# Regrouping one search's VectorE work into fewer slots in step 1 of an adjacency-attention kernel

## Chip, core and metric

The kernel runs on one core of a Trainium2 chip. The metric is the time of one execution on the device in microseconds (us); the time of a kernel is the median of its runs. Work is issued to five engines, each with its own queue taken in order: TensorE (PE, with its weight loads shown apart as PEld), VectorE (DVE), ScalarE (ACT), GpSimd (POOL) and SyncE (SP, which here only starts DMAs).

## What is computed

Two layers over 2708 nodes with 256 features. The part that the change touches is in layer 0, which does this twice (step 0, step 1), with `Xf = Xa = X` at first:

```python
R = S + eye;  R = R / R.sum(-1, keepdims=True)      # S: the 2708 x 2708 adjacency
for n in range(2):
    A  = top_p_attention(Xa, W1, W2, W3)            # softmax rows, kept to 90% of their mass
    Xf = R @ Xf
    Xa = A @ Xa
    Z  = Z + Xf @ U1[n].T + Xa @ U2[n].T
# then a layernorm; layer 1 is a 4-head masked attention over the same graph, and a layernorm
```

`top_p_attention` sorts each row of probabilities in descending order, keeps entries until the sum before an entry reaches 0.9, sets the others to zero and divides by the sum that is left. So every row needs its own threshold.

## The kernel before

**Tiles and loops.** The 2708 rows are cut into 22 tiles, 16 of 128 rows and 6 of 110. In each of the two steps a loop over the 22 tiles (`step`) does the product `A @ Xa` of one tile: in six groups of up to four column blocks, PE transposes the block of the tile's probabilities `e` (L269), ACT copies the result out of PSUM as `eT` (L274), and PE multiplies it with the values into the bank `att` (L287). After each group `between` calls `slot` once. So there are six slots to a tile, and a slot is the unit of the hand-written order.

**What a slot issues** (`slot`, in this order): one more part of each search that is under way, the oldest search first; one part of each row-wise job that is under way (`doing`: layernorms and sums of finished rows; a layernorm here is L136, L138, L140 and L144 on DVE and L142 on POOL); the start of a new search, where one is due; and 11 or 12 matmuls of the *walk*. PE, ACT, DVE and POOL are in manual order (`engines`, in `tc.manual_schedule`): each does its instructions in the order in which the generators issued them. SP is not in that set: a planner of the language puts its DMAs in order, by when it expects each to be ready.

**The walk** (`walks`) is `R @ Xf` for both steps. It is one long stream that starts at the end of step 0's attention and ends at the end of step 1's. For each of 11 pairs of tiles it makes seven products of 11 matmuls each (L1136), which are combined later. The products share two PSUM banks in most of the stream. Each product must be read out before the next but one can use its bank: products 1, 2 and 5 by ACT (L1144, L1150, L1152), products 6, 7, 4 and 3 by DVE (L1146, L1148, L1154, L1156). A readout is issued with the last matmul of its product, so on DVE it stands behind the search work of its slot. L1158 and L1160 are two short reciprocals of the walk.

**A search** (`search`) finds the threshold of one tile. Each `yield` in it ends its part for the present slot. In step 1 its parts are, with the slots counted from the search's start:

- slots 0 and 1, `scores`: logits on PE (L798), exponentials on ACT (L817); a few sums on POOL
- slots 1 to 5, `survey`: four passes over `e` on ACT (L840, 2.64 us each) and short POOL instructions between them (L849 to L872)
- slot 6, `bound`: ten short DVE instructions, then one pass over 2708 columns (L905) that writes `scr`
- slots 7 and 8, `candidates`: 28 MAX8 instructions on DVE (L920), 14 in each slot, which take the eight largest of each of 28 pieces
- slot 9, first part of `settle`: the sort (L933 to L940: six MAX8 and five MATCH_REPLACE8 over 224 candidates) and the sums (L942 to L949)
- slot 10: counts of ties (L958 to L979)
- slot 11: seven MATCH_REPLACE8 over `e` (L986), which write `key`
- slot 12: the last masking of `e` (L989) and a reciprocal (L992); then the tile is ready

A new search starts every tile, in the slot after group 4 (the fifth of the tile), for the tile three ahead. So three searches overlap, one of them at slot k + 6 when another is at slot k. The last masking of a tile is issued in the fifth slot of the tile before it, and the first transposes of the masked tile come in the PE queue right behind that slot's walk matmuls. Before the loop of step 1 starts, a stretch without attention issues 15 slots with 14 walk matmuls each, in which the first three searches of step 1 start.

In step 0 the same functions run with `s == 0`: no `survey`, no `bound`, no ties.

Of the kernel before, what the change touches and what calls it, by code (L numbers as in the profile page):

```python
# [47 lines left out]
def kernel(  # L48
# [506 lines left out]
    def fast_layer0(ep, adjp):  # L555
# [17 lines left out]
        parts = (CHUNKS_0, CHUNKS_1)  # L573
# [258 lines left out]
        def new(name, m):  # L832
            return small.tile([P, 1], F32, name=name)[:m]
# [78 lines left out]
        def candidates(s, t, src):  # L912

            m = rows[t]
            size = -(-N // parts[s])
            cand = sortp.tile([P, CHUNKS_1, 8], F32, name="cand")[:m, : parts[s]]
            for n in range(parts[s]):
                if n == parts[s] // 2:
                    yield
                nc.vector.max(cand[:, n, :], src[:m, n * size : min(N, (n + 1) * size)])  # L920
            return cand

        def settle(s, t, e, cand, tau):

            m = rows[t]  # L930
            want = sorted_[s]
            _, nxt, most, above, left = (f[:m, t : t + 1] for f in facts[s])
            nc.vector.tensor_reduce(most, cand[:, :, 7], axis=AX.X, op=ALU.max)  # L933
            flat = cand.rearrange("p n k -> p (n k)")
            work = sortp.tile([P, CHUNKS_1 * 8], F32, name="work")[:m, : parts[s] * 8]
            top = sortp.tile([P, SORTED_0], F32, name="top")[:m, :want]
            for k in range(0, want, 8):
                nc.vector.max(top[:, k : k + 8], work if k else flat)
                if k + 8 < want:
                    nc.vector.match_replace(work, top[:, k : k + 8], work if k else flat, 0.0)  # L940
            sums = sortp.tile([P, SORTED_0], F32, name="sums")[:m, :want]
            nc.vector.tensor_tensor_scan(sums, top, top, 0.0, op0=ALU.add, op1=ALU.max)  # L942
            nc.vector.scalar_tensor_tensor(
                sums, sums, tau, top, op0=ALU.subtract, op1=ALU.is_ge, accum_out=left
            )
            nc.vector.tensor_tensor_reduce(
                sums, sums, top, 1.0, 0.0, op0=ALU.mult, op1=ALU.max, accum_out=nxt
            )
            nc.vector.tensor_scalar(  # L949
                sums, top, nxt, None, op0=ALU.is_gt, op1=ALU.add, accum_out=above  # L950
            )
            key = e
            if s:
                yield

                need = new("need", m)
                upto = small.tile([P, SEGS], F32, name="upto")[:m]
                nc.vector.tensor_add(need, above, left)  # L958
                nc.vector.tensor_scalar(
                    need, need, -1.0, float(want), op0=ALU.mult, op1=ALU.add  # L960
                )
                nc.vector.tensor_scalar(work, flat, nxt, None, op0=ALU.is_equal)
                nc.vector.tensor_reduce(
                    haves[:m, t], work.rearrange("p (s k) -> p s k", s=SEGS),
                    axis=AX.X, op=ALU.add,
                )
                nc.vector.tensor_tensor_scan(
                    upto, haves[:m, t], haves[:m, t], 0.0, op0=ALU.add, op1=ALU.max
                )
                nc.vector.tensor_sub(upto, haves[:m, t], upto)  # L970
                nc.vector.tensor_scalar(wants[:m, t], upto, need, None, op0=ALU.add)
                few = sortp.tile([P, SEGS, 8], F32, name="few")[:m]
                none = sortp.tile([P, SEGS, 8], F32, name="none")[:m]
                nc.vector.tensor_tensor(
                    few, place[:m].unsqueeze(1).to_broadcast([m, SEGS, 8]),
                    wants[:m, t].unsqueeze(2).to_broadcast([m, SEGS, 8]), op=ALU.is_lt,
                )
                nc.vector.tensor_scalar(none, few, -1.0, None, op0=ALU.add)
                nc.vector.scalar_tensor_tensor(  # L979
                    few, few, nxt, none, op0=ALU.mult, op1=ALU.add  # L980
                )
                yield
                key = wk.tile([P, N], F32, name="scr")
                for k in range(SEGS):
                    cut = slice(k * seg, min(N, (k + 1) * seg))
                    nc.vector.match_replace(key[:m, cut], few[:, k, :], e[:m, cut], 3e38)  # L986
            yield
            den, rden = new("den", m), new("rden", m)
            nc.vector.scalar_tensor_tensor(  # L989
                e[:m], key[:m], nxt, e[:m], op0=ALU.is_gt, op1=ALU.mult, accum_out=den  # L990
            )
            nc.vector.reciprocal(rden, den)  # L992
            return rden

        def search(s, t):

            e, z, tau = yield from scores(s, t)
            if s:
                seen = yield from survey(t, e, z, tau)
                src, rest = bound(t, e, z, tau, *seen)  # L1000
            else:
                src, rest = e, tau
            yield
            cand = yield from candidates(s, t, src)
            yield
            ready[t] = e, (yield from settle(s, t, e, cand, rest))
# [897 lines left out]
```

## Time and profile before

| | |
|---|---|
| median of 3 runs | 1517.05 us (1516.17 to 1520.15) |
| the profiled execution | 1516.33 us, of which the span is 1514.5 us |
| mean granted TensorE clock | 0.994 |
| PE busy over the span | 1485.1 us (98%) |
| DVE busy | 1282.9 us (85%) |
| ACT busy | 808.8 us (53%) |
| POOL busy | 596.7 us (39%) |

By stretch, from the span's start: step 0's attention runs from about 66 us to 430 us; the stretch between the steps to about 500 us; step 1's attention to 1178 us; layer 1 to the end. Busy time of 100 us in three stretches of step 1:

| stretch | PE | DVE | ACT | POOL |
|---|---|---|---|---|
| 500 to 600 us | 99.97 | 82.11 | 58.24 | 24.93 |
| 800 to 900 us | 99.41 | 91.32 | 63.29 | 51.93 |
| 1000 to 1100 us | 98.65 | 91.92 | 63.38 | 48.64 |

An engine's share of the whole span says little about one stage; the table by stretch and the list of who waits for whom say more. The layernorms of finished rows run on DVE and POOL only from about 800 us on, since they need the second walk.

### The profile page before, as it was taken

The numbers are of one execution on the slowest core, as the hardware profiler recorded it, in microseconds if no ns is written. First come the engines' busy times: TensorE is split into PE (matmuls) and PEld (weight loads), VectorE is DVE, ScalarE is ACT, GpSimd is POOL, SyncE is SP. The second block draws the span as 40 slices with busy tenths as digits, with TensorE's granted clock in tenths as the row PEclk, the third lists the DMA queues.
The fourth block names the chain that finished last, engine by engine and source line by source line (L and its number), as shares of the span: only waits on it lengthen the run. The fifth ranks groups of instructions, "written<-read, shape, count | busy, mean of one in ns | idle before, by whom it ended". The sixth has DMA issues, their size and how long they took to land. (4 is left out here: it accounts for less than half of the span.)

```text
span 1514.5 us, 30074 instructions
## 1 busy us (share of the span) xinstructions
PE 1485.1 (98%) x10547; PEld 1068.2 (71%) x10547; DVE 1282.9 (85%) x3750; ACT 808.8 (53%) x1535; POOL 596.7 (39%) x978
## 2 busy tenths in 40 slices
PE   9999999999999999999999999999989999999996
PEld 5477777777788889888888888888879333333343
DVE  4589999999516978888899988999986998999996
ACT  3444544454336456655665666665643444456474
POOL 0066775765023322222355544544552210045133
PEclk9999999999999999999999999999999999999998
DMA  6478988885048555545665555655455555334331
GB/s 182 142 251 271 292 260 256 257 234 177 12 136 264 165 173 180 165 131 146 183 192 157 172 170 173 181 168 161 149 167 142 153 143 164 101 106 133 89 106 53
DMA packets 214265, 255.92 MB, mean 169 GB/s; under 512 B 41921, under 2 KB 180317, under 8 KB 214105
## 3 DMA queue, kind: packets, MB, share of 16 engines
q1 hardware_dynamic: 203638, 245.31, 54.4%
q10 hardware_dynamic: 10467, 8.60, 1.8%
q8 instruction: 85, 1.39, 0.4%
q14 instruction: 75, 0.61, 0.1%
HBM read 190.03 MB, written 62.44 MB: 167 GB/s over the span
## 5 line engine op out<-in xcount | busy, mean ns | idle before, releaser
L274 ACT COPY eT<-tr 128x512 f32<-128x512 f32 (+5 forms) x264 | 141.7, 537 | 229.4 <-PE tr L269 226.6
L840 ACT ACTIVATE junk<-e,minus,rth 128x2708 bf16<-128x2708 f32 (+1 forms) x88 | 232.9, 2646 | 48.3 <-POOL rth L872 47.5
L287 PE MATMUL att<-ba,eT 128*128 128x256 f32 (+3 forms) x968 | 231.5, 380 | 0.0
L287 PE MATMUL att<-xm,eT 128*128 128x256 f32 (+3 forms) x968 | 230.8, 379 | 0.3 <-ACT xa L1374 0.3
L1691 PE MATMUL acc<-pt,v 128*32 128x512 f32 (+3 forms) x2112 | 217.0, 543 | 0.4
L1679 DVE SCALAR_TENSOR_TENSOR pt<-e,tj,blk 128x1024 f32<-128x1024 f32 (+3 forms) x176 | 184.1, 1110 | 6.0 <-ACT blk L251 2.7
L287 PEld LDWEIGHTS att<-ba,eT 128*128 128x128 f32 (+3 forms) x968 | 170.2, 187 | 21.6
L287 PEld LDWEIGHTS att<-xm,eT 128*128 128x128 f32 (+3 forms) x968 | 169.5, 186 | 22.0 <-ACT xa L1374 0.7
L1136 PEld LDWEIGHTS walk<-xe,blk 128*128 128x128 f32 (+1 forms) x1386 | 164.3, 187 | 13.7 <-issue 10.7
L1136 PE MATMUL walk<-xe,blk 128*128 128x128 f32 (+3 forms) x1386 | 173.3, 275 | 0.5 <-ACT u_sb L1144 0.4
L1691 PEld LDWEIGHTS acc<-pt,v 128*32 128x32 f32 (+1 forms) x2112 | 71.4, 110 | 126.6 <-issue 91.5
L269 PE MATMUL tr<-ident,e 128*128 128x128 f32 (+3 forms) x968 | 147.1, 271 | 2.0 <-ACT eT L274 1.4
L817 ACT ACTIVATE e<-lg 128x1024 f32<-128x1024 f32 (+3 forms) x112 | 106.6, 957 | 67.3 <-PE lg L798 64.7
L269 PEld LDWEIGHTS tr<-ident,e 128*128 128x128 f32 (+3 forms) x968 | 113.4, 139 | 32.8 <-issue 14.0
L1136 PE MATMUL walk<-xm,blk 128*128 128x128 f32 (+3 forms) x1034 | 131.6, 277 | 3.0 <-DVE xw L1156 1.7
L1136 PEld LDWEIGHTS walk<-xm,blk 128*128 128x128 f32 (+3 forms) x1034 | 124.8, 188 | 13.2 <-issue 6.5
L1701 PE MATMUL acc<-pt,sb 128*32 128x512 f32 (+3 forms) x1056 | 113.8, 542 | 0.0
L1679 DVE SCALAR_TENSOR_TENSOR pt<-r,tj,blk 128x1024 f32<-128x1024 f32 (+1 forms) x88 | 109.9, 1312 | 1.3 <-PE acc L1701 0.5
L920 DVE MAX8 cand<-e 128x8 f32<-128x170 f32 (+1 forms) x352 | 86.0, 320 | 24.5 <-ACT e L817 16.2
L250 ACT ACTIVATE blk<-blk 128x1024 f32<-128x1024 f32 (+3 forms) x66 | 63.3, 960 | 77.8 <-DMA blk<-in_adjT_dram 71.7
L920 DVE MAX8 cand<-scr 128x8 f32<-128x97 f32 (+1 forms) x616 | 102.8, 244 | 0.0
L824 POOL TENSOR_TENSOR fact<-zp 128x1 f32<-128x1 f32 (+1 forms) x44 | 40.0, 909 | 136.0 <-ACT e L817 135.9
(298 smaller groups left out, 2488.4 us busy)
## 6 DMA issues: line engine op xcount, KB each, us to landing
blk<-in_adjT_dram SPq DMA_DIRECT2D x68, 512.0 KB
blk<-S SPq DMA_DIRECT2D x48, 512.0 KB
blk<-D SPq DMA_DIRECT2D x24, 512.0 KB
blk<-in_adjT_dram SPq DMA_DIRECT2D x26, 440.0 KB
D<-blk SPq DMA_DIRECT2D x16, 512.0 KB
S<-scr SPq DMA_DIRECT2D x16, 512.0 KB
S<-blk SPq DMA_DIRECT2D x16, 512.0 KB
xm<-S SPq DMA_DIRECT2D x16, 512.0 KB
```

Source lines behind the costliest of these rows:

```text
L250: nc.scalar.activation(bar, bar, AF.Sign)
L269: nc.tensor.transpose(tr[: rows[t], q, :m], e[:m, off[t] : off[t + 1]], ident[:m, :m])
L274: copy(eT[:k, : len(grp), :m], tr[:k, : len(grp), :m])
L287: nc.tensor.matmul(acc, eT[: rows[t], q, :m], value(t), start=(t == 0), stop=(t == NT - 1),)
L817: nc.scalar.activation(halves[:m, :, c0 : c0 + w], lg[:m, :, :w], AF.Exp, accum_out=zp[:m, n : n + 1],)
L824: nc.gpsimd.tensor_add(z, zp[:m, 0:1], zp[:m, 1:2])
L840: nc.scalar.activation(junk[:m], e[:m], func, scale=rth, bias=minus1[:m], accum_out=acc)
L920: nc.vector.max(cand[:, n, :], src[:m, n * size : min(N, (n + 1) * size)])
L1136: nc.tensor.matmul(ac, blk[:k, j, :], MOVING[name](j, k, w), start=start and j == 0, stop=j == PAIRS - 1, skip_group_check=True,)
L1679: nc.vector.scalar_tensor_tensor(pt[:k, :gw], targets[g][h // 2][:k, h % 2, :gw], tj[:k, j, h : h + 1], bar, op0=ALU.max, op1=ALU.mult,)
L1691: nc.tensor.matmul(acc[h // 2][c][to : to + SIDE, :w], v[j][:k, h, o : o + SIDE], probs[n][h][:k, c0 : c0 + w], **at,)
L1701: nc.tensor.matmul(acc[2][c][h * SIDE : (h + 1) * SIDE, :w], sb[:k, j, h : h + 1].to_broadcast([k, SIDE]), probs[n][h][:k, c0 : c0 + w], **at,
```

## The change

```diff
@@ candidates
             for n in range(parts[s]):
-                if n == parts[s] // 2:
+                if n == parts[s] // 2 and not s:
                     yield
                 nc.vector.max(cand[:, n, :], src[:m, n * size : min(N, (n + 1) * size)])
@@ settle
                 if k + 8 < want:
                     nc.vector.match_replace(work, top[:, k : k + 8], work if k else flat, 0.0)
+            if s:
+                yield
             sums = sortp.tile([P, SORTED_0], F32, name="sums")[:m, :want]
             nc.vector.tensor_tensor_scan(sums, top, top, 0.0, op0=ALU.add, op1=ALU.max)
@@ settle
             key = e
             if s:
-                yield
-
                 need = new("need", m)
```

In step 1 the 28 MAX8 of a search are issued in one slot instead of two; a slot ends between the sort and the sums; and no slot ends between the sums and the counts of ties. The parts from slot 6 on become:

| slot of the search | before | after |
|---|---|---|
| 6 | bound | bound |
| 7 | 14 MAX8 | 28 MAX8 |
| 8 | 14 MAX8 | sort |
| 9 | sort, sums | sums, ties |
| 10 | ties | MATCH_REPLACE8 over `e` |
| 11 | MATCH_REPLACE8 over `e` | last masking |
| 12 | last masking | (ready) |

No instruction is added or removed on any engine. The order on PE, ACT and POOL stays as it was, and so does that of the DMAs that ACT starts. The order on DVE changes as in the table. The planner of SP's queue also moves some DMAs past each other, all from step 1's attention on, but for one pair before it: stores of finished rows (L1322) and loads of row tiles (L1089, L1090, L1094) change places with loads of walk blocks (L693, L681); and at the end of step 1 the first three loads of layer 1's values (L1667, tiles 8, 9 and 10) come ahead of its first mask load (L248) and of two loads of `e` (L228), and wait for DVE there. Step 0 keeps its slots. Lines are numbered as in the kernel before.

## The prediction

> **What bounds the kernel.** I read the page first: busy time, then the slices.
>
> ```profile
> PE 1485.1 (98%) x10547; PEld 1068.2 (71%) x10547; DVE 1282.9 (85%) x3750; ACT 808.8 (53%) x1535; POOL 596.7 (39%) x978
> ...
> PE   9999999999999999999999999999989999999996
> ...
> DVE  4589999999516978888899988999986998999996
> ```
>
> PE has no room nearly everywhere, and DVE is second, with the least room in the second half of step 1 (slices of 37.9 us; 20 to 30 are 757 to 1174 us). The change leaves PE's instructions and their order alone. So it can only gain what PE waits now, and what follows from such waits. The list of PE's waits from 500 to 1180 us has it whole (columns: engine and line, what it waited for, us in total, times, longest):
>
> ```profile
> PE walk L1136 <- DVE xw L1154: 3.5, 1, 3.5
> PE walk L1136 <- DVE xw L1156: 1.7, 1, 1.7
> PE tr L269 <- ACT eT L274: 1.4, 2, 0.8
> PE lg L798 <- ACT cs L184: 1.2, 2, 1.0
> PE walk L1136 <- ACT u_sb L1144: 1.1, 2, 0.7
> PE tr L269 <- DVE e L989: 0.6, 1, 0.6
> PE walk L1136 <- DVE u_sb L1148: 0.6, 1, 0.6
> PE lg L174 <- ACT xT L170: 0.6, 1, 0.6
> ```
>
> With 0.2 left out these are 10.7 us. DVE has a part of 6.4 us: one wait for the masking, and three for a bank of the walk that DVE had not read out. The same list before 500 us has one more, 1.3 us for L1146 at 485 us. The largest comes at the end, in the timeline from 1112 to 1136 us (start, us, engine):
>
> ```profile
> 1122.02 3.03 DVE L989 SCALAR_TENSOR_TENSOR e<-scr,fact,e 110x2708 f32<-110x2708 f32 x1
> ...
> 1128.10 3.47 DVE L905 SCALAR_TENSOR_TENSOR scr<-e,hi 110x2708 f32<-110x2708 f32 x1
> ...
> 1132.21 0.28 DVE L1154 TENSOR_TENSOR xw<-walk,u_sb 110x128 f32<-110x128 f32 x1
> ```
>
> The last masking of one search and the pass of the next one's bound stand in the same slot; the readout L1154, whose product had ended at 1124.36, stands behind both. PE sat from 1129.02 to 1132.54. Last, the granted clock by stretch (stretch, its length, PE busy, clock, DMA):
>
> ```profile
> 1128.00:1132.00 4.00, 1.02 (x10) 1.00 0.86 228
> 1132.00:1134.00 2.00, 1.46 (x7) 0.55 1.09 300
> 1134.00:1136.00 2.00, 2.00 (x7) 0.59 0.69 221
> 1136.00:1138.00 2.00, 2.00 (x14) 1.00 0.05 15
> ```
>
> After that wait PE got half its clock: (0.45 + 0.41) x 2 us / 0.5 = 3.4 us of it, which is 1.7 us lost. The 1.74 us wait that ended at 500.03 has the same behind it (0.69, 0.50 and 0.96 in the 2 us stretches from 500 us: 3.4 us). The 1.27 us wait at 485 us has not.
>
> [...]
>
> **The change, part by part.** Nothing is added, so the account is one of places in DVE's queue. Lengths of the parts, from DVE's timeline around 500 us, where no layernorms lie between: masking 3.24 us, bound 5.13, 14 MAX8 2.34, sort 5.08, sums 1.13, ties 2.47, MATCH_REPLACE8 over e 3.80. Together 25.5. Taking slots modulo six, since a search at slot 12 meets the next at slot 6, DVE got per slot 8.4, 2.3, 2.3, 6.2, 2.5, 3.8 and will get 5.1, 4.7, 5.1, 3.6, 3.8, 3.2. A tile takes PE about 30 us (equal logits follow at 30.2 us at 557 and 587), so a slot is some 5 us: the heap of 8.4 goes. Seen from the start of the bound's slot, DVE's work up to the end of each slot changes by -3.3, -0.9, +1.9, -0.7, +0.6, 0. Readouts behind the bound come earlier; those behind the sort come later.
>
> I laid DVE's rows out in the new order with these lengths, each readout no earlier than its product's end, each layernorm no earlier than POOL's part had been, and the bound no earlier than its last ACT pass had been, and compared each end with the time at which PE starts the next product in that bank.
>
> *Between the steps* (468 to 511 us DVE never idles). After the bound's readout at 473.8, 28 MAX8 end at 478.4; L1154, which was at 476.06, comes then and PE, which wants the bank at 478.05, waits 0.7. Sort, sums and ties follow before L1146: 478.44 + 0.28 + 5.08 + 1.13 + 2.47, less some overlap, gives 487.2 instead of 484.79, so that wait grows from 1.27 to 2.9. The 1.74 at 498 goes, as PE is late anyhow; L1156 stays at 499.69. Then L1146 behind the next sort, 510.0 instead of 504.91, costs 0.5. Net +0.7 + 2.9 - 1.27 - 1.74 + 0.5 = **+1.1**. The clock falls once in either order, since 2.9 is longer than 1.74. Bounds: -0.8 if the first two waits are half as long, +2.8 if the clock falls a second time.
>
> *At 901 us*: L1148 stood behind masking and bound, and PE waited from 901.27 to 901.88. Laid out it comes at 901.32 instead of 901.54, for DVE now sorts where it idled 2.9 us at 875; with PE 1.1 us later from the stretch above, nothing waits. **-0.6**, bounds 0 and -0.6.
>
> *Masking*, a slot earlier: the wait of 0.6 before L269 at 1125.20 goes, **-0.6**. The mask would have to be later by a slot to cost again.
>
> *At 1129 us*: DVE idled 4.1 us at 1105 waiting for a product; the sort now fills this. Masking is done before the last ACT pass of the next search ends (1122.63), so the bound is the first to wait: its rest from L893 took 6.5 us, L1154 is ready near 1129.9 instead of 1132.5. **-2.8** of 3.5. What is late next is ACT's pass, not DVE. Bounds 0 and -3.5.
>
> *The clock there*: 0.7 us of waiting is less than the 1.27 that brought no fall: **-1.7**, bounds 0 and -1.7.
>
> *Waits for ACT*, 4.3 in the list: ACT stood behind its own passes (L840), which waited for POOL (L872), and POOL for layernorms on DVE. The layernorm in the slot after the sort keeps its place within 1 us as laid out, but near 1111 it comes 1.8 earlier, so the 0.8 at 1120 goes: **-0.8**. The others I cost at nothing; bounds -4.3 and +4.3, as much again.
>
> *Readouts that come later* are covered by their banks' slack. The least is left at 786 us (L1146 comes 3.0 later, slack 3.0), at 824 (1.6 against 1.7), at 911 (L1154, 4.4 against 5.2) and at 1047 (0.1 against 0.6). I take **+0.5**, bounds 0 and +3.
>
> *SP's queue* changes places too. A store L1322 now ahead of walk blocks can hold them until its layernorm ends. Blocks are started three products ahead, some 15 us, and PE waited for a block 0.5 us in the whole stream. The values' loads now ahead of the first layer 1 mask wait for DVE; the last masking, at 1154.56 before, is earlier now, and the mask's load started at 1154.34. **0**, bounds -0.5 and +2.
>
> *Layer 1* begins as much earlier as PE ends step 1; its first weights (L1679) ran 6.6 us before PE's first use. 0.
>
> Sum: +1.1 - 0.6 - 0.6 - 2.8 - 1.7 - 0.8 + 0.5 = -4.9. The profiled execution took 1516.33 us (span 1514.5 and 1.8 around it), 0.7 below the median, so 1511.4 there and **1512.1** for a median.
>
> **Rivals.** *The tail wait stays* (25%): the bound stretches with late layernorms and ACT, as L905's 3.47 and a 6.8 us bound there show, so L1154 gains 1 us or less and the clock still falls. +1.1 - 1.2 - 1.0 + 0.5: 1516.4. This is also how it looks if parting the search moves no critical readout. *ACT's waits go as well* (10%): a smoother DVE frees POOL and so ACT everywhere. Against it: POOL is late by itself (L1162 took 3.12 us at 491.69 beside a masking, and 0.46 at 468.33). -4.9 less another 3.5: 1508.6. *Slower* (15%): the readout behind 28 MAX8 or the whole sort. Place: the four tight banks named. Were DVE 2 us slower there than laid out, as that bound was by 1.7, the waits are 2.0, 1.9, 1.2 and 1.5, and one fall of the clock 1.7: 8.3; with between the steps +1.1, and -1.2 kept: 1517.05 + 8.2 = 1525.2. It decides from about 1 us of extra lag on.
>
> **Numbers.** My forecast has 50%. 0.3%, about what a measurement of this kernel can tell from no change, is 4.55 us, so the line lies at 1512.5, hardly above the forecast: of its 50, 32 fall below and 18 within. With the ACT case faster is 42; same is 18 + 25 + 2 of the slower case, 45; slower 13. The range, 1507.5 to 1519, leaves out most of the slower case and the end of the ACT case.
>
> **What will show it.** Right: no PE wait for L1154 over 1 us near 1130, full clock there, a 2 to 3 us wait for L1146 near 485 us and none near 498; DVE idling short before bounds for ACT. Wrong: waits for L1146 or L1148 near 786, 824 or 1047 us, more waits for ACT's eT, or DMA waits of the walk. The total depends on the tail's clock more than on all small waits.

## The result, and the profile after

The changed kernel took 1523.04 us (median of 9 runs, 1518.06 to 1527.94), the kernel before 1517.05 (9 runs, 1514.30 to 1520.15): a ratio of 1.0037, 95% interval 1.0023 to 1.0051. The forecast was 1512.1, with a range of 1507.5 to 1519. So it went the other way. On another chip, later, the same pair gave 1521.28 against 1518.89, 1.0006 [0.9986, 1.0025], so no difference is shown there: the runs of both kernels are spread over 9 to 11 us, the longer ones at a lower granted clock (1516.09 us at 0.995, 1524.24 us at 0.992); the profiles below show one reason for it in the changed kernel, and no long run of the kernel before was profiled.

The profiled execution took 1522.55 us, with a span of 1520.7. First its page, busy time and the slices:

```profile
PE 1488.5 (98%) x10547; PEld 1077.8 (71%) x10547; DVE 1288.5 (85%) x3750; ACT 808.4 (53%) x1535; POOL 595.7 (39%) x978
...
PE   9999999999998999999999999999999999999996
...
DVE  4589999999516978888899987999897998999996
```

At this grain nothing has happened: the same engines, the same shares. 6 us in 1520 do not show in slices of 38 us. The list of PE's waits from 500 to 1180 us does show it:

```profile
PE walk L1136 <- ACT u_sb L1144: 3.3, 1, 3.3
PE tr L269 <- ACT eT L274: 3.1, 3, 2.2
PE walk L1136 <- DVE xw L1154: 2.6, 1, 2.6
PE lg L798 <- ACT cs L184: 1.2, 2, 1.0
PE walk L1136 <- DVE xm L1031: 0.4, 1, 0.4
PE lg L174 <- ACT xT L170: 0.3, 1, 0.3
```

The waits for DVE fell from 6.4 to 3.0 us here (L1156's, L1148's and the mask's are gone, L1154's is 2.6 for 3.5); one more, for L1146, lies at 485 us and is 3.7 for 1.3. But the waits for `eT` and L1144 on ACT, 1.4 and 1.1 before, are now 3.1 and 3.3, and each has a long one: 2.2 us at 895 and 3.3 us at 931. The timeline from 884 to 897 us says what stands behind the first (start, us, engine, line):

```profile
888.49 0.22 POOL L870 TENSOR_SCALAR g<-g 128x1 f32<-128x1 f32 x1
888.63 3.03 DVE L989 SCALAR_TENSOR_TENSOR e<-scr,fact,e 128x2708 f32<-128x2708 f32 x1
...
888.79 3.29 POOL L871 TENSOR_TENSOR g<-g,power 128x1 f32<-128x1 f32 x1
...
892.16 0.19 POOL L872 TENSOR_TENSOR rth<-rth,g 128x1 f32<-128x1 f32 x1
...
892.38 2.64 ACT L840 ACTIVATE junk<-e,minus,rth 128x2708 bf16<-128x2708 f32 x1 [7.37 <-POOL rth L872]
...
895.02 0.56 ACT L274 COPY eT<-tr 110x512 f32<-110x512 f32 x1
...
895.64 0.52 PE L269 MATMUL tr<-ident,e 128*110 128x128 f32 x2 [2.22 <-ACT eT L274]
```

Read it from the bottom. PE waited for a copy of `eT`; the copy stood behind a pass of the next search's survey on ACT; the pass had waited 7.37 us for `rth` from POOL (L872); and POOL stood in L871, a POW on 128 numbers, for 3.29 us, until DVE's last masking was over. The masking had begun 0.16 us before it. In the kernel before, at the same point of the work:

```profile
887.64 0.56 POOL L871 TENSOR_TENSOR g<-g,power 128x1 f32<-128x1 f32 x1
...
888.50 2.64 ACT L840 ACTIVATE junk<-e,minus,rth 128x2708 bf16<-128x2708 f32 x1 [4.86 <-POOL rth L872]
...
892.25 3.03 DVE L989 SCALAR_TENSOR_TENSOR e<-scr,fact,e 128x2708 f32<-128x2708 f32 x1
```

L871 took 0.56 us, and the masking came 4.6 us later. A slot is about 5 us: the change moved the masking from slot 12 to slot 11, that is from beside slot 6 of the next search to beside its slot 5, and there the chain L866 to L872 of that search (issued in slot 4) is still running on POOL. It is late: ACT's part was there at 882.1 us, but row sums (L1315 to L1318) of finished rows kept POOL busy until 887.3. 34 us on, the same once more, in the timeline from 918 to 933 us:

```profile
922.71 3.03 DVE L989 SCALAR_TENSOR_TENSOR e<-scr,fact,e 128x2708 f32<-128x2708 f32 x1
...
922.98 3.18 POOL L871 TENSOR_TENSOR g<-g,power 128x1 f32<-128x1 f32 x1
...
926.46 2.64 ACT L840 ACTIVATE junk<-e,minus,rth 128x2708 bf16<-128x2708 f32 x1 [5.83 <-POOL rth L872]
...
930.82 2.50 PE L1136 MATMUL walk<-xe,xm 128*128 128x128 f32 x10 [3.35 <-ACT u_sb L1144]
```

And behind each wait PE's clock fell (stretch, length, PE busy, clock, DMA):

```profile
896.00:898.00 2.00, 2.00 (x6) 0.50 0.77 289
898.00:900.00 2.00, 2.00 (x8) 0.68 0.26 76
...
930.00:932.00 2.00, 1.18 (x5) 0.50 0.84 294
932.00:934.00 2.00, 2.00 (x12) 0.50 0.47 135
934.00:936.00 2.00, 2.00 (x11) 0.50 0.23 56
```

The clock was at half for 3.4 us and for 6.8 us; by the delay of PE's own instructions this cost 1.7 and 2.7 us, as part of the second fall lay in the wait itself. The account by the starts of the walk's products, after less before: +1.3 us from 506 to 895, +4.6 at 907, +10.1 at 940, +10.0 at 1125, +5.8 when the walk ends. So the two collisions cost 8.7 us, and the tail gave back 4.2. A third masking meets the chain at 546 us (L867 takes 2.92 us for 0.19), and no wait of PE follows there.

So beside a masking of 3.03 us L871 took 3.29 and 3.18 us, where it took 0.56 in the kernel before. The prediction left such a meeting out, though it quoted L1162 with 3.12 us beside a masking and 0.46 elsewhere.

### The profile page after: what moved, and what is told of

It reads as the page before. It is cut to its first block, busy times and chain, and to the rows that moved or that the text cites. A ratio compares the mean times of both kernels' runs of the same rounds, so it can differ in the third digit from the quotient of the medians.

```text
span 1520.7 us, 30061 instructions
## 1 busy us (share of the span) xinstructions
PE 1488.5 (98%) x10547; PEld 1077.8 (71%) x10547; DVE 1288.5 (85%) x3750; ACT 808.4 (53%) x1535; POOL 595.7 (39%) x978
## 5 line engine op out<-in xcount | busy, mean ns | idle before, releaser
L1679 DVE SCALAR_TENSOR_TENSOR pt<-e,tj,blk 128x1024 f32<-128x1024 f32 (+3 forms) x176 | 184.1, 1110 | 6.1 <-ACT blk L251 2.7
L1136 PEld LDWEIGHTS walk<-xe,blk 128*128 128x128 f32 (+1 forms) x1386 | 164.3, 187 | 13.9 <-issue 10.7
L1136 PE MATMUL walk<-xe,blk 128*128 128x128 f32 (+3 forms) x1386 | 173.3, 276 | 0.8 <-DVE xw L1154 0.4
L1691 PEld LDWEIGHTS acc<-pt,v 128*32 128x32 f32 (+1 forms) x2112 | 75.3, 110 | 122.9 <-issue 89.7
L1136 PE MATMUL walk<-xm,blk 128*128 128x128 f32 (+3 forms) x1034 | 132.5, 279 | 3.7 <-DVE u_sb L1146 3.7
L1136 PEld LDWEIGHTS walk<-xm,blk 128*128 128x128 f32 (+3 forms) x1034 | 125.6, 190 | 13.6 <-issue 7.3
L824 POOL TENSOR_TENSOR fact<-zp 128x1 f32<-128x1 f32 (+1 forms) x44 | 33.9, 770 | 143.6 <-ACT e L817 143.6
```

The source lines that it names most:

```text
L824: nc.gpsimd.tensor_add(z, zp[:m, 0:1], zp[:m, 1:2])
L1136: nc.tensor.matmul(ac, blk[:k, j, :], MOVING[name](j, k, w), start=start and j == 0, stop=j == PAIRS - 1, skip_group_check=True,)
L1679: nc.vector.scalar_tensor_tensor(pt[:k, :gw], targets[g][h // 2][:k, h % 2, :gw], tj[:k, j, h : h + 1], bar, op0=ALU.max, op1=ALU.mult,)
L1691: nc.tensor.matmul(acc[h // 2][c][to : to + SIDE, :w], v[j][:k, h, o : o + SIDE], probs[n][h][:k, c0 : c0 + w], **at,)
```

## The experiments

**Theory 1**: the cost is the masking on POOL's chain; POOL, then ACT, then PE are late, and the clock falls. **Theory 2**, the prediction's own rival: 28 MAX8 in a row, or a whole sort, hold up readouts on DVE. Two numbers are told of each kernel: its time against the kernel before, measured beside it, and, from its profile, how much longer the walk's stretch of step 1 (430 to 1165 us) is than in the first profile of before, "step 1" for short. The second is needed because seven of the sixteen profiles lost 4 to 8 us ahead of step 1, in code that all these kernels share: PE waited there for a mask of step 0. One of them, the list of waits from 300 to 360 us:

```profile
PE tr L269 <- DVE e L993: 3.4, 1, 3.4
```

No profile of before or of the changed kernel has it. What brings it was not settled.

### The parts alone

The masking back in slot 12, the rest of the change kept:

```diff
             yield
+            if s:
+                yield
             den, rden = new("den", m), new("rden", m)
```

> The changed kernel with one more slot between MATCH_REPLACE and the last masking of step 1: the 28 MAX8 in one slot and the parted sort stay, the masking goes back to the slot it had before. Theory 1 (the masking, a slot sooner, stands beside the younger search's chain on POOL; its POW at L871 is held for the masking's length, 3.2 us where it took 0.56, and ACT's pass and PE's operands follow late): L871 takes about 0.6 us again near 888 and 922 us, PE's waits of 2.2 us at 895 and 3.35 us at 930 go, with the two stretches of half clock behind them (3.4 and 6.8 us), so about 9 us come back up to 1100 us; the wait for L1154 near 1135 grows to 3.5 us again. Time 1514 to 1519, at least 4 below the changed kernel. Theory 2 (the 28 MAX8 in a row, or the whole sort, hold up layernorm parts and readouts on DVE, and POOL and ACT are late by that): the waits at 895 and 930 stay, and the time is that of the changed kernel or above, 1522 to 1527.

1524.99 us, ratio 1.0040 [1.0024, 1.0056]; step 1 +4.6. L871 took 0.6 us at both places, and the waits at 895 and 930 went down to 0.7 at most, with no fall of the clock: so far theory 1. But the time did not fall. Its list of waits from 780 to 1100 us (lines are two higher: L1148 is L1146 of before, L1150 is L1148):

```profile
PE walk L1138 <- DVE u_sb L1150: 1.9, 3, 1.1
PE tr L269 <- ACT eT L274: 1.4, 2, 1.2
...
PE walk L1138 <- DVE xm L1035: 0.8, 1, 0.8
...
PE walk L1138 <- DVE u_sb L1148: 0.4, 1, 0.4
```

L1148 and L1150 are readouts, at 818, 828, 1015 and 1053 us (L1035, at 782, is an operand of the walk that DVE makes), by the kind of tight bank that the "slower" rival named (786, 824, 911, 1047). With the masking back in the bound's slot, 28 MAX8 and the parted sort cost by theory 2. The changed kernel has none of these waits, so there it is not theory 2.

The masking sooner alone, from the kernel before, which needs a slot: MATCH_REPLACE8 goes into the slot of the ties.

```diff
                     few, few, nxt, none, op0=ALU.mult, op1=ALU.add
                 )
-                yield
                 key = wk.tile([P, N], F32, name="scr")
```

> The kernel before with one edit: MATCH_REPLACE goes into the slot of the ties, so that the masking stands a slot sooner, where the change put it; the MAX8 stay halved and the sort and sums together. Theory 1: the masking alone is what costs; L871 is held about 3 us beside a masking again, PE waits 2 us or more for ACT's eT or u_sb somewhere from 880 to 940 us, and the time is at least that of before, 1517 to 1524. Theory 2: no such waits, since neither the MAX8 nor the sort are moved: 1511 to 1517.

1530.25 us, 1.0066 [1.0041, 1.0091]; step 1 +9.7. Slower than either theory said, and not for the reason of theory 1: no L871 was held (L870 was, 3.02 us at 551, and PE did not wait behind it). Ties and MATCH_REPLACE8 in one slot hold the readout that follows (L1147 here is L1148 of before):

```profile
PE walk L1135 <- DVE u_sb L1147: 6.2, 3, 2.2
PE walk L1135 <- DVE xw L1155: 3.2, 2, 2.1
PE walk L1135 <- DVE xw L1153: 2.5, 1, 2.5
...
```

The edit that made room for the masking cost more than what it was to test. It tells nothing for or against theory 1.

The sums back with the sort, the other two parts kept:

```diff
-            if s:
-                yield
             sums = sortp.tile([P, SORTED_0], F32, name="sums")[:m, :want]
...
             if s:
+                yield
                 need = new("need", m)
```

> The changed kernel with one of its three parts undone: the sums go back into the slot of the sort, and the ties have a slot of their own again; 28 MAX8 in one slot and the masking a slot sooner stay. Theory 1 (masking beside POOL's chain): L871 is held about 3 us at 888 and perhaps at 923 us, PE waits 2 us or more for ACT's eT or u_sb at 895, as in the changed kernel; time 1516 to 1528, as there. Theory 2 (the whole sort holds readouts up): with 1.1 us more behind each sort, waits for L1146 and L1148 appear or grow between 780 and 1060 us, where the changed kernel has none above 0.5, and the time is 3 us or more above the changed kernel's.

1521.73 us, 1.0046 [1.0028, 1.0065]; step 1 +4.5. L871 took 3.29 at 889.5 and 3.24 at 923.7, PE waited 2.2 and 3.4 us, the clock fell at 897.0 and 931.1: theory 1. The waits for L1146 and L1148 in between are 0.6 at most, so theory 2 adds little.

The first two searches in their old places:

```diff
-                if n == parts[s] // 2 and not s:
+                if n == parts[s] // 2 and (not s or t < 2):
...
-            if s:
+            if s and t >= 2:
                 yield
...
             if s:
+                if t < 2:
+                    yield
                 need = new("need", m)
```

> The changed kernel, but the first two searches of step 1 keep the old places (MAX8 halved, sums with the sort, masking last), so that only the stretch between the steps is as before. Both theories: the wait of 3.7 us for L1146 near 485 us goes, the waits of before (1.3 at 485, 1.7 at 498) come back, and up to 880 us the kernel is level with before, some 1.3 us sooner than the changed kernel. Theory 1: from there on it is the changed kernel: L871 held about 3 us at 888 or 923, PE waits of 2 to 3.4 us behind it, and the clock falls behind those waits or not; in two profiles of the changed kernel this gave 8.7 and 2.3 us. Theory 2: the waits at 895 and 930 do not depend on the masking and POOL; with PE 1 us earlier they are readouts. Time 1516 to 1526, median 1 to 3 below the changed kernel.

1518.63 us, 1.0013 [1.0000, 1.0027]; step 1 -0.9. Level with before up to 895 us, as expected; there L871 took 3.29 and PE waited 2.2 us, but the clock stayed up, and at 920.06 L871 took 0.57.

### The same kernels again

> The kernel before, unchanged, for a second profile, on the chip that takes the other kernels. The profiles so far show two kinds of executions that have nothing to do with step 1: in three of the experiments PE waited 3 to 6 us for a mask of step 0 near 335 us and lost 4 to 8 us there, in before, in the changed kernel and with the masking late it did not. Both theories: step 1 looks as in the first profile, with waits of 1.3, 1.7 and 3.5 us near 485, 498 and 1130, L871 at 0.6 us near 887 and 918; the wait near 335 may or may not be there. Time 1514 to 1524.

1516.66 us; step 1 within 0.1 us of the first profile. L871 0.6 us, waits 1.6, 1.8 and 3.5.

> The changed kernel, unchanged, for a second profile beside before on the same chip. Theory 1: L871 is held near 3 us again at about 889 and 923 us, PE waits 2 us or more near 895 and 930, and the clock is halved behind both. Theory 2: the place of the long waits differs from profile to profile, and where they are it is a readout (L1146 to L1156) that PE waits for. Time 1520 to 1528.

1516.21 us, 6.3 below the first profile of the same kernel; step 1 +0.3. L871 is held at 888.09 (3.29 us) and PE waits 2.3 us at 895, but no fall of the clock follows (stretch, length, PE busy, clock, DMA):

```profile
896.00:898.00 2.00, 2.00 (x10) 1.00 0.75 273
```

And the second collision is missed:

```profile
920.64 0.57 POOL L871 TENSOR_TENSOR g<-g,power 128x1 f32<-128x1 f32 x1
...
921.51 2.65 ACT L840 ACTIVATE junk<-e,minus,rth 128x2708 bf16<-128x2708 f32 x1 [3.25 <-POOL rth L872]
...
922.37 3.03 DVE L989 SCALAR_TENSOR_TENSOR e<-scr,fact,e 128x2708 f32<-128x2708 f32 x1
```

L871 is 1.7 us ahead of the masking here and was 0.3 behind it in the first profile.

> The changed kernel, unchanged, timed beside the other three on one chip. Both theories: 1521 to 1525 for the median, some runs near 1516 to 1518. Theory 1: its profile has L871 at 3.3 us near 888 and the 2.2 us wait at 895; a second held L871 near 923 and a wait of 3.3 us near 930 only if the clock fell at about 896.

1521.28 us (12 runs, 1516.09 to 1524.76); profiled at 1516.09, and like the second profile: step 1 +0.1, L871 3.29 us at 888.2 and 0.57 at 920.7, a wait of 2.2 and no fall at 896. With the two kernels above that have the same masking, five profiles: in two the clock fell behind the first wait, and in both L871 was held again at 923; in three it did not fall, and in none of them was it. All five have the first collision.

### Is it the two inputs?

The masking reads two operands of 2708 columns from SBUF, `scr` and `e`, and takes 3.03 us; the two inputs or the length could be what holds L871. Here it is replaced by a comparison with one SBUF input, run twice; the multiplication by `e` is left out.

```diff
-            nc.vector.scalar_tensor_tensor(
-                e[:m], key[:m], nxt, e[:m], op0=ALU.is_gt, op1=ALU.mult, accum_out=den
-            )
+            if s:
+                for k in range(2):
+                    nc.vector.tensor_scalar(
+                        e[:m], key[:m], nxt, None, op0=ALU.is_gt, op1=ALU.add, accum_out=den
+                    )
```

> The changed kernel with another instruction in the masking's place: a comparison of e's key with the bound that reads one operand from SBUF and not two, run twice so that DVE is busy about as long. It leaves out the multiplication by e, so the weights are 0 and 1 and the output is not the reference's; the order and all else stay. Theory 1, in the form that an instruction of DVE with two inputs from SBUF keeps POOL out while it runs: L871 takes about 0.6 us at 888 and 923 though DVE is busy beside it, long instructions on POOL beside the masking (16 in the changed kernel) go, PE's waits at 895 and 930 stay below 1 us. If any long instruction of DVE keeps POOL out, L871 still takes as long as one of the two beside it lasts. If theory 2 holds, waits at 895 and 930 stay. The time: 1512 to 1520 by theory 1, should the pair be as long as the masking was.

1534.96 us, 1.0096 [1.0066, 1.0126]. The time was mis-expected: one instruction takes 3.03 us with one input as with two, so the pair is 6.1 us and DVE is late everywhere. What it was for is plain in the timeline from 899 us:

```profile
899.81 3.03 DVE L991 TENSOR_SCALAR_CACHE_REDUCE e<-scr,fact 128x2708 f32<-128x2708 f32 x1
899.97 0.56 POOL L871 TENSOR_TENSOR g<-g,power 128x1 f32<-128x1 f32 x1
...
900.83 2.64 ACT L840 ACTIVATE junk<-e,minus,rth 128x2708 bf16<-128x2708 f32 x1 [5.84 <-POOL rth L872]
```

L871 again begins 0.16 us after a DVE instruction of 3.03 us, and takes 0.56; PE's waits there are 0.7 us. Over step 1, 45 instructions of POOL began during the 133 us of one-input instructions, and none took over 0.8 us longer than usual for its line; in the changed kernel 14 began during the 66.6 us of maskings, and 13 did. In the run with one input the bound's pass (L905), which reads `e` twice and has the masking's form, still held POOL: 15 began beside it, and 10 took over 0.8 us longer. So it is not the length. One input and two also differ in the form of the instruction here, and no run parts the two.

### The masking in four pieces

```diff
+            if s:
+                each = -(-N // 4)
+                dens = small.tile([P, 4], F32, name="dens")[:m]
+                for k in range(4):
+                    cut = slice(k * each, min(N, (k + 1) * each))
+                    nc.vector.scalar_tensor_tensor(
+                        e[:m, cut], key[:m, cut], nxt, e[:m, cut],
+                        op0=ALU.is_gt, op1=ALU.mult, accum_out=dens[:, k : k + 1],
+                    )
+                nc.vector.tensor_reduce(den, dens, axis=AX.X, op=ALU.add)
```

> The changed kernel with the last masking of step 1 cut into four pieces by columns (four instructions of about 0.85 us instead of one of 3.1, and a small sum of their four denominators); the order is untouched. Theory 1: POOL gets in between two pieces, so L871 takes at most about 1.5 us beside a masking; PE's waits at 895 and 930 us shrink below 1 us and the clock keeps up there. With the tail's gain kept, 1510 to 1516. Theory 2: pieces of the same total length change nothing: 1522 to 1526, some 0.5 us of more work on DVE per search included.

> The changed kernel with the masking of step 1 in four pieces, for a second profile: in the first one the waits at 895 and 930 us were gone and step 1 cost no more than in before, but its time was 1524 to 1528, 8 us of it from a wait for a mask of step 0 near 335 us. Theory 1 holds for step 1 if it is again within 2 us of before's step 1. If instead step 1 is 5 us or more longer here, with the waits at 895 and 930 or others in their place, pieces do not mend what the change did. Time 1516 to 1526.

The timeline from 898 to 903 us:

```profile
898.48 0.92 DVE L994 SCALAR_TENSOR_TENSOR e<-scr,fact,e 128x677 f32<-128x677 f32 x1
...
898.63 1.18 POOL L871 TENSOR_TENSOR g<-g,power 128x1 f32<-128x1 f32 x1
...
899.31 0.92 DVE L994 SCALAR_TENSOR_TENSOR e<-scr,fact,e 128x677 f32<-128x677 f32 x1
...
900.32 2.65 ACT L840 ACTIVATE junk<-e,minus,rth 128x2708 bf16<-128x2708 f32 x1 [5.47 <-POOL rth L872]
```

L871 waits for one piece, not for the masking: 1.18 us. The wait at 895 is gone, the one at 930 is 0.8, and step 1 is -0.3 and +1.4 in two profiles, within the 2 us of theory 1. The time is not: 1525.88 us, 1.0046 [1.0028, 1.0063], with 1524.23 and 1526.51 for the profiled runs. Both lost 8.1 and 7.2 us near 335 us, ahead of step 1.

> The changed kernel with the first two searches of step 1 in their old places and the masking of step 1 in four pieces: the two stretches in which the changed kernel lost time, between the steps and from 880 to 940 us, undone together, its tail kept. Theory 1: no L871 over 1.5 us, no PE wait over 1 us from 520 to 1100 us, and step 1 ends 2 to 4 us sooner than in before; 1513 to 1517 where step 0 is undisturbed, 4 to 8 more where PE waits for a mask near 335 us. Theory 2: no better than the first two in their old places alone, 1517 to 1520.

The same with the first two searches in old places: profiled at 1517.23 us without that loss in step 0; step 1 -1.2, no wait over 1.2 us from 520 to 1120. The median is 1524.02, 1.0029 [1.0012, 1.0046], so it fails as a remedy: ten of its twelve runs lie above 1520, and there is no profile of one of those.

### Only the two collisions undone

```diff
             yield
+            if s and t in (13, 14):
+                yield
             den, rden = new("den", m), new("rden", m)
```

> The changed kernel, but the searches of tiles 13 and 14 do their last masking a slot later, where before had it: these two of the 22 are the maskings that began at 888.6 and 922.7 us, 0.2 us ahead of POOL's L871 (or in its way) in the changed kernel. Nothing else moves. Theory 1: L871 takes 0.6 us at both places, PE's waits of 2.2 at 895 and 3.3 at 930 us go to 0.8 or less, and what these stretches cost (8.7 us in one profile of the changed kernel, 2 in the other) is saved, less 0.5 to 1 for the bound that now follows a masking in two slots: 1515 to 1519, at least 3 below the changed kernel on the same chip. Theory 2 (readouts behind 28 MAX8 or the whole sort): no change from the changed kernel, within 1.5 us.

1516.63 us against 1521.28 of the changed kernel on the same chip, 0.9990 [0.9970, 1.0010] of before; step 1 -2.8. Moving 2 of 22 maskings takes 4.7 us off the median and 2.9 off the mean of twelve runs (95% interval by resampling the runs: 0.3 to 5.5). In the profiles step 1 is 2.9 us shorter than in the changed kernel on that chip, 2.4 of it by 907 us. The timeline from 886 us, where the masking is L991:

```profile
888.61 0.56 POOL L871 TENSOR_TENSOR g<-g,power 128x1 f32<-128x1 f32 x1
...
889.48 2.64 ACT L840 ACTIVATE junk<-e,minus,rth 128x2708 bf16<-128x2708 f32 x1 [4.66 <-POOL rth L872]
...
892.03 3.03 DVE L991 SCALAR_TENSOR_TENSOR e<-scr,fact,e 128x2708 f32<-128x2708 f32 x1
```

The waits there are 0.7 us at most, and no fall follows. Theory 2 expected no change. It falls for this kernel.

> The changed kernel with the two maskings of tiles 13 and 14 a slot later and the first two searches of step 1 in their old places: both stretches where the changed kernel lost, undone by moves alone. Theory 1: between the steps as in before, no wait over 1 us from 520 to 1120 us, the tail with a wait of 2.7 us and its gain of 1.7 to 2.4: 1513 to 1517, 1 to 3 below before on the same chip and 2 to 4 below the first two in old places alone. Theory 2: as the first two in old places alone, 1517 to 1520.

1515.79 us, 0.9972 [0.9954, 0.9991]; step 1 -3.6: both stretches mended, as expected.

### A place without the collision

One more slot ahead of the bound, so that all from the bound on stands a slot later; the 28 MAX8, the parted sort and the distance from bound to masking are the change's.

```diff
                 seen = yield from survey(t, e, z, tau)
+                yield
                 src, rest = bound(t, e, z, tau, *seen)
```

> The changed kernel with one more slot between the survey and the bound of step 1's searches: everything from the bound on stands a slot later, so the masking is at its old distance from its own walk and the MAX8, sort and sums, ties and MATCH_REPLACE keep slots of their own. Modulo six the masking then stands beside the next search's survey and no longer beside the bound, or the slot ahead of it. Theory 1: what decides is whether the masking's 3.1 us fall on POOL's chain of the younger search (L866 to L872) at the start of a slot; here it shares the slot with that chain as it did before, so L871 stays short, ACT is not late at 895 and 930, time 1511 to 1518. Theory 2: the 28 MAX8 are still in one slot and the sort in another, so the waits stay: 1521 to 1526.

> The kernel with the bound a slot later, on the chip of the other three. Both theories: 1511 to 1520 as before, 3 to 5 us below the kernel before and 7 to 9 below the changed kernel; L871 at 0.6 us near 888 and 921.

1514.68 us, 0.9969 [0.9954, 0.9984], and 1512.09, 0.9957 [0.9933, 0.9981]: faster than both kernels. Step 1 is -5.9 and -6.3. The list of waits from 500 to 1180 us of the second (lines from the bound's call on are one higher: L1137 is L1136 of before):

```profile
PE tr L269 <- DVE e L989: 2.2, 2, 1.5
PE lg L798 <- ACT cs L184: 1.2, 2, 1.0
PE walk L1137 <- ACT u_sb L1145: 1.1, 2, 0.7
...
```

Per slot DVE has the same loads as in the changed kernel, one slot later against the walk and against POOL: the masking stands beside slot 6 of the next search again, when L871 is over (0.56 us at 889), and now without the bound. The mask itself is late at the tail, 2.2 us, but there is no wait for L1154, and 4.5 us of the gain over before come after 1110 us. Ahead of that list, near 487 us, PE no longer waits for L1146 but 2.4 and 2.1 us for a block of the walk, with a fall of the clock behind it; why the block is late was not settled.

> The kernel with the bound a slot later (masking where it was, 28 MAX8 and parted sort kept), and the masking in four pieces as well. Theory 1: there the masking does not meet POOL's chain, so pieces have nothing to mend; each search has about 0.5 us more to do on DVE and the mask that PE waits for at the tail (2.2 us) comes so much later: 1514 to 1518, against 1511 to 1520 (median 1514.7) in one piece. If pieces free POOL and ACT in general, it is 3 us or more below the one in one piece, 1509 to 1512.

1516.49 us, 0.9984 [0.9970, 0.9998]; step 1 -6.8, with 7.8 lost near 335. Pieces have nothing to mend here, as theory 1 said.

## Why the prediction was wrong

**Waits for ACT: the step that failed.** "The others I cost at nothing; bounds -4.3 and +4.3". In the result's profile these waits came to 7.9 us instead of 4.3. That growth lies within the bounds; but two waits, at 895 and 931 us, grew by 4.8, and the half clock behind them, another 4.4 us, stood in no term. At 901 us the forecast had -0.6; measured from 895 to 940 is +8.7 in the result's profile, 9.3 apart, and +1.8 and +1.9 in the two milder ones. The layout moved DVE's rows and kept POOL's: "each layernorm no earlier than POOL's part had been". Nothing asked which POOL instruction would now stand beside a masking. The row with the price was in the text (L1162, 3.12 us for 0.46), used only to doubt a gain.

**Between the steps**: +1.1 forecast; +1.4 in the result's profile, +0.9 in the other two. The wait for L1146 was 3.5 to 3.7, not 2.9, and in the result's profile the clock was at half for 6.8 us behind it instead of 3.4, but the net was right.

**At 901 us, and later readouts**: where the collisions are undone -0.6 at 902, as forecast, then +1.1 up to 1093 for +0.5, of which 0.4 is a longer wait for ACT (L174) and not a readout.

**The tail**: forecast -5.9 (-0.6 for the mask, -2.8, -1.7 for the clock, -0.8 for ACT); measured -4.2 in the result's profile and with the collisions undone, -2.5 in the milder profiles of the changed kernel. The readout itself came as laid out:

```profile
1134.97 3.04 DVE L905 SCALAR_TENSOR_TENSOR scr<-e,hi 110x2708 f32<-110x2708 f32 x1
...
1139.53 0.28 DVE L1154 TENSOR_TENSOR xw<-walk,u_sb 110x128 f32<-110x128 f32 x1
...
1139.86 0.47 PE L1136 MATMUL walk<-xe,xm 128*110 128x128 f32 x2 [2.64 <-DVE xw L1154]
```

Less the 10.0 us that PE was late by then, L1154 stood at 1129.5, for a forecast of 1129.9. But PE stood there at 1137.2, or 1127.2, and not at 1129.0: 1.8 us sooner, 1.4 of it because the waits of 0.6 and 0.8 just ahead had gone. So it waited for the same readout 2.6 us and not 0.7, and the 1.4 us were counted twice. And behind such a wait, of 2.6 to 2.7 us, the clock fell in the two milder profiles, not in the result's nor where the collisions were undone. That the clock kept up in these two was luck: it hung on when the wait began (the larger piece of it was 1.66 and 1.65 us, last section).

**The sum**: in the kernel with two maskings moved the stretches are +0.9, -0.6, +1.1 and -4.2, or -2.8, and its profiled run took 1513.65 us, 2.7 below the first of before. The forecast's -4.9 less the 1.4 counted twice is -3.5. So most of the reckoning held in that profile, which had the luck of the clock at the tail; in the medians the gain is not clear of noise (0.9990). One cost that was not asked for turned the forecast round.

**The rivals**: "the tail wait stays" was partly so. "Slower" had the sign and the wrong place: its tight banks did cost, but in other kernels, above all with the masking back in the bound's slot; in the changed kernel PE waits for no readout by DVE from 780 to 1100 us.

## What to carry to other kernels

When work is moved to another slot, list what then runs beside it on the other engines, not only what stands behind it in its own queue; here L871, of 0.56 us, took 3.18 to 3.29 us when it began beside a masking of 3.03 us that reads two operands from SBUF, and ACT and PE waited for it in turn (7.37 and 2.22 us at the first place). Two waits on one path are not two gains: when the first goes, the second can grow by as much (1.4 us here). And if the same load can be put a slot earlier or later against the rest, try both, since the phase may decide more than the balance.

## What had not been expected of the hardware

- The same wait of 2.2 to 2.3 us at 895 was followed by a fall of the clock to half in two profiles and not in three, and the wait of 2.6 to 2.7 us at the tail by one in four profiles and not in two (the result's and that with two maskings moved). Its length alone did not tell; its place did. In each of the 18 profiles the falls begin whole multiples of 3.413 us apart (in the result's profile at 486.25, 895.85 and 929.98 us: 120 and 10 of them; in the first of before at 500.75 and 1132.22 us: 185), and within the work they lasted one or two of these, 3.41 or 6.83 us.
- Cut each profile at these points and add up PE's idle time in each piece of 3.413 us that began at full clock, from 66 to 1480 us. All 37 pieces with 1.86 us or more ended in a fall (2.51, 2.22 and 2.51 us in the result's profile, 3.19 in the first of before), none with 1.66 us or less did, and of the eight between, from 1.73 to 1.82 us, two did (one is the wait of 1.74 us at 498 in the first of before). At 895 the wait lay whole in one piece in the two profiles with the fall (2.22 and 2.23 us); in the three without, such a point cut it, and the larger part was 1.29, 1.16 and 1.44 us. At the tail it lay whole in one piece four times; in the two profiles without a fall the larger part was 1.66 and 1.65 us.
- One fall went with the next in all five profiles: where it came at 896, L871 met the next masking at 923 (3.18 and 3.24 us), and where it did not, L871 took 0.57 us there. So one kernel had profiled runs of 1516.2 and 1522.6 us.
- A pass over 2708 columns took DVE 3.03 us with one input from SBUF as with two; beside it L871 took 0.56 us with one, and 3.18 to 3.29 with two.
